# A fused attention and state-space kernel: the block hand-over spread over the chunks, weights scaled earlier, and attention's stages moved against the scans

## The chip, the cores and the metric

The kernel runs on one core of a Trainium2 chip. The metric is the device time of one execution in microseconds (us); below 0.2% two kernels of this kind can't be told apart. In the trace the engines are PE (matrix multiply), PEld (its weight loads), DVE (vector), ACT (activation functions), POOL (general purpose, elementwise here) and SP (which only issues DMA transfers here).

## What is computed

The input `x` is 8 samples of 512 channels by 48 x 48 = 2304 places, float32. Two layers follow one another, each of the form `x = x + layer(group_norm(x))`.

- Layer 0 is causal linear attention with 8 heads of 64 channels: `Q` and `K` are `elu(.) + 1` of linear maps of the input, `V` is a linear map; each place sums `k v^T` over all places up to it, multiplies by its `q`, and divides by `q` times the running sum of `k`.
- Layer 1 cuts the 512 channels into 4 blocks of 128 that depend on each other: a block's input is its own slice plus the output of the block before. Each block is a Mamba layer with 256 inner channels and 16 states: a convolution over 4 places with `silu`, a step size `delta = softplus(...)`, the recurrence `h = exp(delta*A)*h + delta*x*B` over 2304 places for every pair of channel and state, the output `sum(C*h)`, a gate `silu(z)` and a projection. Its result `x_m` is fused with the block's input `x_i`:

```
fused_global = max(x_i, x_m)
w_local, w_global = sigmoid(mean(x_i)), sigmoid(mean(fused_global))
fused = w_local * x_i + w_global * fused_global
```

The means run over all places, so a block's fusion can begin only when its last chunk is done, and the next block needs it.

## The kernel before

**Tiling.** 2304 places are 6 chunks of 384. One block of one sample over one chunk is a `Job`; there are 8 x 4 x 6 = 192. Two streams of jobs (even and odd samples) are interleaved in a fixed order, so that between the last chunk of a block and the first chunk of the next block of the same stream two jobs of the other stream run. A job is 8 slots. In a slot DVE makes the products of the next slot (`product`, L795) and runs 4 scans (`scan`, L816), each of 128 rows by 384 places; ACT makes for each scan the decay `exp(delta*A)` (`decay`, L805) in a bank of PSUM; POOL makes the last part of the products (`last_product`, L784) and multiplies the states by `C` (`weigh`, L832); PE sums them into one PSUM tile `yp` (`gather`, L839). The gather of a slot is issued in the middle of the second slot after it. After each half of the channels, in slot 6 and in slot 2 of the next job, DVE multiplies `yp` by the gate (`gated`, L851), and ACT starts `yp` anew (`skip`, L773).

**The order is written out at build time.** Every engine runs its own queue in program order. A planner counts half slots: `beside(half)` is called twice in each slot, before its first scan (even half) and after its second (odd half), and issues what is due from two lists of generators, attention's chunks (`heads`) and all the rest (`tasks`). Each `yield due, banks` says when the next stage may be issued (a number of halves after the last stage, or a fixed half) and how many of the 6 spare PSUM banks it needs; a stage that finds no banks slips to a later half. The decays take from the same 6 banks, 3 in advance (`DEPTH`), up to 5 ahead of silu and softplus. A bank freed by `free(late=True)` is *hot*: its last reader has been issued but is still to run; it is taken only where no other is spare, except by the decays.

**Three kinds of side work** lie beside the scans.

1. `Job.prepare`, once a job, begins 22 halves before the job's first slot: convolution (L624), gate (L635), four silu (L659 to L664), L670, L675, L683, two softplus (L694), POOL's `delta*xs` (L732), DMA loads. Exp, silu and softplus take different tables of ACT, so there is a table load on the way into silu and into softplus, and another back to exp.
2. `chunk(m)`, attention over one chunk, once for each job on the whole. `at(j)` is the half `times[m] + j`. Chunk c of a block has `times = 2 * first slot of the block's first job - BEFORE - (5 - c) * 16`, but at least 11 after the one before it (`DENSE`), and the first of all has `FIRST`. Its stages: projections (L279) at 0, 2 and 4; `q`, `k` (L334, L342); running key sums (L353); `pr` (L363); transposes (L370) at 9 and their copies (L374, L375) at 10; the state matmuls `ds` (L383) at 11 and their sums `S` (L392) at 12; the denominators `den` (L397), `rd` (L400, L402) at 13, `rdb` (L405) at 14; its transposes `rb` (L409) at 15; the product into `q` (L414) at 17; scores (L422) at 18; `sm` (L427) at 20; output matmuls at 21; L443 and L445 at 23. After a block's last chunk `group_norm` turns the statistics into a scale and a bias.
3. `pass_on`, once a block, runs when the block's last job has its maximum (L868). It takes the sums, gets the next block's place (`move_on`, which loads the weights and starts `scale_weights`: `wk` times `wi` on POOL, L493), computes the two sigmoids (L537 to L540, the sums at L549 and L552), and then fuses the 6 chunks one after another, each in 4 halves: ACT L579, L580, L584, POOL L589, L594, L597. The conv stage of a job waits in the planner until its chunk of the stream's input is ready and `st.scaled` is set.

Halves are counted below within a job: half 0 is the start of its slot 0, half 14 the start of its slot 7. Job starts are multiples of 16 halves, so stage `at(j)` of a chunk that isn't pushed by `DENSE` falls on half (j - BEFORE) modulo 16.

Of the kernel before, what the change touches and what calls it, by code (L numbers as in the profile page):

```python
# [9 lines left out]
F32 = mybir.dt.float32  # L10
# [6 lines left out]
P = 128  # L17
# [11 lines left out]
BEFORE, PERIOD, DENSE, FIRST = 62, 16, 11, -110  # L29
# [20 lines left out]
def attention_then_mamba_kernel(  # L50
# [111 lines left out]
    def group_norm(stats, n, name, bufs):  # L162


        bank = Banks()
        yield "1", 1
        mv = small.tile([P, n, 2], F32, tag=f"mv{n}", name=f"mv_{name}", bufs=1)
        for ct in range(n):
            nc.vector.bn_aggr(mv[:, ct, :], stats[:, ct].rearrange("p c s -> p (c s)"))
        mean_ps = bank()  # L170
        nc.tensor.matmul(mean_ps[:, 0:n], grp, mv[:, :, 0], start=True, stop=True)
        yield "1", 0
        gm = small.tile([P, 3, n], F32, tag=f"gm{n}", name=f"gm_{name}", bufs=1)
        nc.vector.tensor_copy(gm[:, 0, :], mean_ps[:, 0:n])
        bank.free()
        nc.vector.tensor_sub(gm[:, 1, :], mv[:, :, 0], gm[:, 0, :])
        nc.vector.tensor_mul(gm[:, 2, :], gm[:, 1, :], gm[:, 1, :])
        nc.vector.tensor_add(gm[:, 2, :], gm[:, 2, :], mv[:, :, 1])
        yield "0", 1
        var_ps = bank()  # L180
        nc.tensor.matmul(var_ps[:, 0:n], grp, gm[:, 2, :], start=True, stop=True)
        yield "1", 0
        nc.vector.tensor_scalar_add(gm[:, 2, :], var_ps[:, 0:n], 1e-5)
        bank.free()
        norm = small.tile([P, 3, n], F32, tag=f"norm{n}", name=f"norm_{name}", bufs=bufs)
        nc.gpsimd.tensor_tensor(norm[:, 0, :], gm[:, 2, :], power[:, 0:n], ALU.pow)
        yield "1", 0
        nc.vector.scalar_tensor_tensor(
            norm[:, 1, :], gm[:, 0, :], -1.0, norm[:, 0, :], ALU.mult, ALU.mult
        )  # L190
        nc.vector.scalar_tensor_tensor(
            norm[:, 2, :], gm[:, 1, :], float(L), norm[:, 0, :], ALU.mult, ALU.mult
        )
        return norm
# [64 lines left out]
    def chunk(m):  # L259
# [35 lines left out]
        if o == 0:  # L295
            yield at(-4), 0
            while b not in norms or m not in fetched:
                yield "1w", 0
            xn, norm = fetched.pop(m), norms[b]
            for ct in range(4):  # L300
                if ct:
                    yield at(ct - 4), 0
                nc.gpsimd.tensor_scalar(
                    xn[:, ct, :],
                    xn[:, ct, :],
                    norm[:, 0, ct : ct + 1],
                    norm[:, 1, ct : ct + 1],
                    ALU.mult,
                    ALU.add,
                )  # L310
            save(xns[b].rearrange("(t p) l -> p t l", p=P)[:, :, cols], xn)
        yield at(0), 1
# [64 lines left out]
        yield at(11), 1  # L377

        more = NT if c + 1 < NC else NT - 1
        ds = bank()[:, 0 : NT * 64].rearrange("p (i d) -> p i d", i=NT)  # L380
# [3 lines left out]
        yield at(12), 0  # L384
# [9 lines left out]
        yield at(12, 0), 1  # L394
        den = bank()[:, 0 : 2 * NT]
        for i in range(NT):
            nc.tensor.matmul(den[:, 2 * i : 2 * i + 2], pr[:, subs[i]], hsel, start=True, stop=True)  # L397
        yield at(13), 0
        rd = small.tile([P, 2 * NT], F32, tag="rd", name=f"rd_{n}", bufs=1)
        nc.vector.tensor_scalar_add(rd, den, 1e-10)  # L400
        bank.free()
        nc.vector.reciprocal(rd, rd)  # L402
        yield at(14), 0
        rdb = new("rdb", 1, (P, 2 * NT, 64))
        nc.scalar.copy(rdb, rd.unsqueeze(2).to_broadcast([P, 2 * NT, 64]))  # L405
        yield at(15), 1
# [5 lines left out]
        yield at(17), 0  # L412
# [5 lines left out]
        yield at(18), 2  # L418
# [4 lines left out]
        yield at(20), 0  # L423
# [6 lines left out]
        yield at(21), 1  # L430
# [11 lines left out]
        yield at(23), 0  # L442
# [9 lines left out]
    class Stream:  # L452


        def __init__(self, z, samples):
            self.z, self.samples = z, samples
            self.xi = cpool.tile([P, 3 + L], F32, name=f"xi_{z}")
            nc.gpsimd.memset(self.xi[:, 0:3], 0.0)
            self.b = None
            self.block = -1  # L460
            self.ready = 0

        def weights(self):

            n, z, s = self.n, self.z, self.s
            wi = wpool.tile([P, 512], F32, tag=f"wi{z}", name=f"wi_{n}")
            nc.sync.dma_start(out=wi, in_=win[s])

            wk = wpool.tile([P, 4, 256], F32, tag=f"wk{z}", name=f"wk_{n}")
            nc.sync.dma_start(  # L470
                out=wk.rearrange("p k d -> p (k d)"), in_=wconv[s].to_broadcast([P, 1024])
            )
            wo = wpool.tile([P, 2, P], F32, tag=f"wo{z}", name=f"wo_{n}")
            nc.sync.dma_start(out=wo, in_=wout[s])
            wx = wpool.tile([P, 2, 40], F32, tag=f"wx{z}", name=f"wx_{n}")
            nc.sync.dma_start(out=wx, in_=wxp[s])
            wd = wpool.tile([64, 256], F32, tag=f"wd{z}", name=f"wd_{n}")
            nc.sync.dma_start(out=wd[32:40, :], in_=wdt[s])
            nc.sync.dma_start(out=wd[40:41, :], in_=bdt[s])
            pv = wpool.tile([P, 4], F32, tag=f"pv{z}", name=f"pv_{n}")  # L480
            nc.sync.dma_start(out=pv[:, 0:2], in_=bconv[s])
            nc.sync.dma_start(out=pv[:, 2:4], in_=dskip[s])
            av = wpool.tile([P, 4, NS // 2], F32, tag=f"av{z}", name=f"av_{n}")
            nc.sync.dma_start(out=av, in_=alog[s])
            self.w = wi, wk, wo, wx, wd, pv, av

        def scale_weights(self):
            wi, wk, wo, wx, wd, pv, av = self.w
            yield "2", 0
            nc.scalar.activation(av, av, AF.Exp)  # L490
            for k in range(4):
                yield "1", 0
                nc.gpsimd.tensor_tensor(wk[:, k, :], wk[:, k, :], wi[:, 0:256], ALU.mult)  # L493
            nc.gpsimd.tensor_scalar_mul(av, av, -1.0)
            self.scaled = True

        def move_on(self):
# [15 lines left out]
            self.weights()  # L513
            self.scaled = False
            tasks.append(Task(self.scale_weights()))

        def pass_on(self):
# [25 lines left out]
            if not last:  # L543
                if self.fresh:
                    self.sums = norm[:, 2, :]
                else:

                    sums = small.tile([P, 2], F32, tag="sums", name=f"sums_{self.n}", bufs=3)
                    nc.vector.scalar_tensor_tensor(  # L549
                        sums[:, 0:1], wt[:, 2:3], wt[:, 0:1], norm[:, 2, :], ALU.mult, ALU.add  # L550
                    )
                    nc.vector.scalar_tensor_tensor(  # L552
# [18 lines left out]
            for c in range(NC):  # L571

                yield "1", 0
# [11 lines left out]
                if old is not None:  # L585
                    yield "1", 0
                    if c + 1 < NC:
                        now = loads(c + 1)
# [10 lines left out]
                else:  # L599
                    yield "1", 0  # L600
                    if c + 1 < NC:
                        now = loads(c + 1)
                self.ready = c + 1

    class Job:
# [6 lines left out]
        def prepare(self):  # L612
# [83 lines left out]
            yield "2", 0  # L696

# [192 lines left out]
    while min(count) < total:  # L890
# [3 lines left out]
        jobs.append(Job(streams[z], count[z], len(jobs) * SLOTS))  # L894
        count[z] += 1
# [200 lines left out]
    with tc.manual_schedule():  # L1096
        half_no[0] = FIRST - 6
        for st in streams:
            tasks.append(Task(st.pass_on()))
# [76 lines left out]
```

## Time and profile before

| | |
|---|---|
| time, median of 3 runs | 9815.3 us (9814.16 to 9816.18) |
| span of the profiled execution | 9811.4 us |
| granted PE clock, mean | 0.905 of full speed |
| DMA, mean | 167 GB/s |
| scans, L816 | 6144 of 941 ns, 5508.1 us |
| products, L795 | 1536 of 1197 ns, 1838.9 us |
| weighing by C, L832 (POOL) | 1536 of 3176 ns, 4878.7 us |
| last products, L784 (POOL) | 1954.2 us |
| decays, L805 (ACT) | 6144 of 580 ns, 3441.7 us |
| ACT table loads, L805, L659 and L694 | 382 + 192 + 192 of 1283 ns |

How to read the profile: its page gives for each engine the time in which it was busy, then 40 equal slices of the span, the DMA queues, the chain of work that ended last, and the costliest groups of instructions by line. Beside the page the trace answers questions: the list of waits names an engine's instruction, whom it waited for, the time in total, how often, and the longest; the groups by shape give busy time and mean of each line; the timeline lists instructions in order of time (start, length, engine, line, operation, operands, how many were merged, and in brackets the idle time ahead of it and who ended it). Neighbouring instructions overlap by some 0.1 us, so busy times of an engine add up to a little more than the time they take.

### The profile page before, as it was taken

How to read it: one execution, taken by the hardware profiler on the slowest of the kernel's cores; microseconds unless marked ns; L12 is line 12 of the kernel's file. 1: busy time of each engine (PE TensorE's matmuls, PEld its weight loads, DVE VectorE, ACT ScalarE, POOL GpSimd, SP SyncE). 2: the span in 40 equal slices, each digit the busy share in tenths (PEclk: the TensorE clock that was granted, in tenths of full speed). 3: DMA queues.
4: the chain of work that ended last, by engine and by line, in shares of the span. 5: the costliest groups of instructions: out<-in, count | busy, mean ns of one | idle time of the engine just before them, and what ended most of it. 6: DMA issues, size and time to landing. Idle time of an engine off the chain costs nothing.

```text
span 9811.4 us, 120393 instructions
## 1 busy us (share of the span) xinstructions
PE 8005.0 (82%) x35714; PEld 3805.1 (39%) x35714; DVE 8465.1 (86%) x11624; ACT 6630.3 (68%) x12624; POOL 8108.8 (83%) x5667
## 2 busy tenths in 40 slices
PE   7888888878888888887888888888888888888865
PEld 4433433333333334333333333433333433334322
DVE  4888888889888888888988888888888888888888
ACT  3666676666776667666677666666666676666666
POOL 3788888888888888888888888888888888888899
PEclk9999999999999999988999999998899999999987
DMA  6566566666666555666666665557666656655555
GB/s 199 154 164 165 160 165 168 171 171 183 175 170 171 160 161 158 169 172 183 177 170 172 167 166 161 161 159 184 179 182 167 165 163 167 170 160 156 163 151 138
DMA packets 1002897, 1642.82 MB, mean 167 GB/s; under 512 B 138592, under 2 KB 797312, under 8 KB 1002240
## 3 DMA queue, kind: packets, MB, share of 16 engines
q1 hardware_dynamic: 1002240, 1635.13, 60.9%
q8 instruction: 282, 4.62, 0.2%
q14 instruction: 375, 3.07, 0.1%
HBM read 1309.06 MB, written 325.58 MB: 167 GB/s over the span
## 4 chain that ended last, share of the span: by engine, by line
DVE 31%; PE 23%; ACT 15%; POOL 11%; issue 9%; DMA 9%; SPq 2%; POOLq 0%; DVEq 0%; ACTq 0%
DVE u L816 20%; PE bank L279 10%; POOL u L832 6%; ACT bank L805 6%; PE yp L839 5%; DVE u L795 5%; PE bank L624 2%; DMA dxr<-xscr 2%; ACT L694 2%; POOL u L784 2%; DMA C<-scr 2%; SPq L724 1%; PE bank L635 1%; PE bank L409 1%; ACT L659 1%
## 5 line engine op out<-in xcount | busy, mean ns | idle before, releaser
L816 DVE TENSOR_TENSOR_SCAN u<-bank,u 128x385 f32<-128x385 f32 (+1 forms) x6144 | 5508.1, 941 | 270.2 <-ACT bank L805 268.6
L832 POOL TENSOR_TENSOR u<-u,C 128x1536 f32<-128x1536 f32 x1536 | 4878.7, 3176 | 463.6 <-DVE u L816 283.7
L805 ACT ACTIVATE bank<-dr,av 128x385 f32<-128x385 f32 (+1 forms) x6144 | 3441.7, 580 | 1618.9 <-DVE u L816 1235.1
L839 PE MATMUL yp<-u,cst 128*64 128x384 f32 x12288 | 2486.2, 527 | 493.7 <-ACT yp L773 264.9
L784 POOL TENSOR_TENSOR u<-B,dxr 128x512 f32<-128x512 f32 x1536 | 1954.2, 1272 | 39.1 <-PE yp L839 24.4
L279 PE MATMUL bank<-xn,wq_sb 128*128 128x384 f32 x4608 | 1908.5, 565 | 20.2 <-DVE fg L868 10.7
L795 DVE TENSOR_TENSOR u<-B,dxp 128x1024 f32<-128x1024 f32 x1536 | 1838.9, 1197 | 13.9 <-ACT dxp L768 11.8
L839 PEld LDWEIGHTS yp<-u,cst 128*64 128x64 f32 x12288 | 797.6, 142 | 1632.2 <-issue 1078.7
L624 PE MATMUL bank<-xi,wk 128*128 128x384 f32 x3072 | 1191.4, 534 | 210.7 <-DVE u L816 162.7
L279 PEld LDWEIGHTS bank<-xn,wq_sb 128*128 128x128 f32 x4608 | 982.3, 224 | 759.3 <-issue 258.7
L830 POOL COPY state<-u 128x4 f32<-128x4 f32 x1280 | 240.9, 188 | 932.0 <-DVE u L816 846.7
L624 PEld LDWEIGHTS bank<-xi,wk 128*128 128x128 f32 x3072 | 603.0, 207 | 854.3 <-DVE u L816 336.7
L291 ACT ACTIVATE ex<-bank,bqkv_sb 128x384 f32<-128x384 f32 x384 | 222.9, 580 | 757.4 <-PE bank L279 738.6
L409 PE MATMUL bank<-cst,rdb 128*128 128x128 f32 x576 | 157.3, 405 | 593.0 <-ACT delta L694 588.9
L851 DVE TENSOR_TENSOR yz<-yp,sz 128x384 f32<-128x384 f32 x384 | 213.3, 556 | 372.6 <-PE yp L839 372.4
L805 ACT ACT_TABLE_LOAD x382 | 490.1, 1283 | 6.7
L732 POOL TENSOR_TENSOR delta<-delta,xs 128x384 f32<-128x384 f32 x384 | 384.1, 1000 | 105.9 <-DMA dscr<-delta 84.4
L635 PE MATMUL bank<-xi,wi 128*128 128x384 f32 x768 | 339.5, 532 | 152.8 <-ACT xs L659 152.8
L392 DVE TENSOR_TENSOR S<-S,bank 128x64 f32<-128x64 f32 x512 | 112.8, 220 | 321.0 <-ACT sz L664 155.6
L348 ACT ACTIVATE vT<-bank,bqkv_sb 128x384 f32<-128x384 f32 x192 | 111.4, 580 | 403.0 <-PE bank L279 403.0
L409 PEld LDWEIGHTS bank<-cst,rdb 128*128 128x128 f32 x576 | 89.1, 196 | 712.9 <-ACT delta L694 684.5
L857 PE MATMUL bank<-yz,wo 128*128 128x384 f32 x768 | 322.6, 542 | 29.2 <-DVE yz L851 12.0
(112 smaller groups left out, 8328.7 us busy)
## 6 DMA issues: line engine op xcount, KB each, us to landing
B<-scr SPq DMA_DIRECT2D x1536, 192.0 KB
C<-scr SPq DMA_DIRECT2D x1536, 192.0 KB
xn<-xn SPq DMA_DIRECT2D x192, 768.0 KB
dr<-dscr SPq DMA_DIRECT2D x768, 192.0 KB
dxr<-xscr SPq DMA_DIRECT2D x768, 192.0 KB
dscr<-delta SPq DMA_DIRECT2D x192, 384.0 KB
xscr<-delta SPq DMA_DIRECT2D x192, 384.0 KB
xn<-in_x SPq DMA_DIRECT2D x48, 768.0 KB
```

Source lines behind the costliest of these rows:

```text
L279: nc.tensor.matmul(ps, wq_sb[:, kt, j * 512 + o * P : j * 512 + (o + 1) * P], xn[:, kt, :], start=(kt == 0), stop=(kt == 3),)
L409: nc.tensor.transpose(rb[:, i, :], rdb[:, 2 * i : 2 * i + 2, :].rearrange("p e d -> p (e d)"), ident)
L624: nc.tensor.matmul(xc, wk[:, k, h * P : (h + 1) * P], xi[:, c0 + k : c0 + k + LC], start=(k == 0), stop=(k == 3),)
L635: nc.tensor.matmul(zp, wi[:, 256 + h * P : 256 + (h + 1) * P], xi[:, c0 + 3 : c0 + 3 + LC], start=True, stop=True,)
L732: nc.gpsimd.tensor_tensor(delta[:, h, :], delta[:, h, :], xs[:, h, :], ALU.mult)
L784: nc.gpsimd.tensor_tensor(u[:, :, :, 1 + LC - TAIL :], self.B[s % 4][:, :, cols].unsqueeze(2).to_broadcast(shape), self.dxr[s // 4][:, :, ...
L795: nc.vector.tensor_mul(u[:, :, :, 1 : 1 + LC - TAIL], self.B[s % 4][:, :, cols].unsqueeze(2).to_broadcast(shape), self.dxp.unsqueeze(1).to ...
L805: nc.scalar.activation(dA[:, cols], self.dr[h][:, g, cols], AF.Exp, scale=self.w[6][:, 2 * h + g, q + j : q + j + 1],)
L816: nc.vector.tensor_tensor_scan(u[:, j, g, cols], dA[:, cols], u[:, j, g, cols], 0.0, ALU.mult, ALU.add,)
L832: nc.gpsimd.tensor_tensor(h, h, self.C[s % 4].unsqueeze(2).to_broadcast([P, NG, 2, LC]), ALU.mult)
L839: nc.tensor.matmul(self.yp[g * 64 : g * 64 + 64, 0:LC], pair_sum, u[:, j, g, 1:], start=False, stop=(s % 4 == 3 and j == NG - 1), skip_gro ...
L857: nc.tensor.matmul(self.xm[:, 0:LC], self.w[2][:, h, :], self.yz[:, h, :], start=(h == 0), stop=(h == 1),)
```

## The change

It has four parts.

1. **Blocks fused chunk by chunk.** `pass_on` no longer runs through the 6 chunks in a burst. From the second chunk on it loads a chunk 36 halves and fuses it 30 halves ahead of the job that needs it; the loads of one chunk are no longer issued while the one before is worked on.
2. **Weights scaled early.** `weights` becomes a task of its own that loads and scales the next block's weights. It starts when the last job of a block has issued its softplus, and not when the block is over. Three tiles that are still in use by then (`wo`, `pv`, `av`) get a second buffer; the multiplication of `av` by -1 goes from POOL to ACT.
3. **Column products with scalars.** In `group_norm` and `pass_on`, products of one column by another (`tensor_mul`, `scalar_tensor_tensor` with two column tensors) become `tensor_scalar`, with the second column as a scalar for each partition. For 4 columns there are 4 such instructions.
4. **Attention's places.** `BEFORE` goes from 62 to 61 and `FIRST` from -110 to -115, so a chunk lies one half later against the jobs. `den` and `ds` go into one bank, in one stage at 12; `rd` and `S` follow in one stage at 14; everything from `rdb` on is one half later again. A new wait at the head of a chunk keeps it behind the chunk two before it.

```diff
-BEFORE, PERIOD, DENSE, FIRST = 62, 16, 11, -110
+BEFORE, PERIOD, DENSE, FIRST = 61, 16, 11, -115
...
-        nc.vector.tensor_mul(gm[:, 2, :], gm[:, 1, :], gm[:, 1, :])
-        nc.vector.tensor_add(gm[:, 2, :], gm[:, 2, :], mv[:, :, 1])
+            nc.vector.tensor_scalar(
+                gm[:, 2, :], gm[:, 1, :], gm[:, 1, :], mv[:, 0, 1:2], ALU.mult, ALU.add
+            )
...
-        nc.vector.scalar_tensor_tensor(
-            norm[:, 1, :], gm[:, 0, :], -1.0, norm[:, 0, :], ALU.mult, ALU.mult
-        )
...
+        for i, factor in ((0, -1.0), (1, float(L))):
+            for ct in range(n):
+                nc.vector.tensor_scalar(
+                    norm[:, 1 + i, ct : ct + 1],
+                    gm[:, i, ct : ct + 1],
+                    norm[:, 0, ct : ct + 1],
+                    factor,
...
+        while read[0] < m - 1:
+            yield "1w", 0
         yield at(0), 1
...
-        yield at(11), 1
+        yield at(12), 1
+        both = bank()
+        den = both[:, 0 : 2 * NT]
+        for i in range(NT):
+            nc.tensor.matmul(den[:, 2 * i : 2 * i + 2], pr[:, subs[i]], hsel, start=True, stop=True)
...
-        yield at(12), 0
+        yield at(14), 0
+        rd = small.tile([P, 2 * NT], F32, tag="rd", name=f"rd_{n}", bufs=1)
+        nc.vector.tensor_scalar_add(rd, den, 1e-10)
+        nc.vector.reciprocal(rd, rd)
...
-        yield at(14), 0
+        yield at(15), 0
         rdb = new("rdb", 1, (P, 2 * NT, 64))
...
-        yield at(15), 1
+        yield at(16), 1
         rb = bank()[:, 0:LC].rearrange("p (i t) -> p i t", i=NT)
...
-            nc.gpsimd.tensor_scalar_mul(av, av, -1.0)
+            nc.scalar.mul(av, av, -1.0)
             self.scaled = True
...
-            self.weights()
-            self.scaled = False
-            tasks.append(Task(self.scale_weights()))
+            self.w = self.coming
...
-                yield "1", 0
+                if c and not last:
+                    first = 2 * self.jobs[self.block * NC + c].start
+                    yield (first - 36, 1), 0
+                    now = loads(c)
+                    yield (first - 30, 1), 0
...
+            if c == NC - 1 and (st.s < 3 or st.samples):
+                tasks.append(Task(st.weights()))
```

## The prediction

> **What bounds the kernel now.** I began with the busy shares on the page, because they tell whether there is a single bound.
>
> ```profile
> PE 8005.0 (82%) x35714; PEld 3805.1 (39%) x35714; DVE 8465.1 (86%) x11624; ACT 6630.3 (68%) x12624; POOL 8108.8 (83%) x5667
> ```
>
> DVE, POOL and PE are all above 80%, so none of them has much to spare. DVE is the fullest, and an average job confirms its lead: 192 jobs of 51 us, of which scans and products take 38. So the question is what DVE waits for. Next I read DVE's rows in the list of waits (total us, times, longest).
>
> ```profile
> DVE yz L851 <- PE yp L839: 372.4, 158, 5.0
> DVE u L816 <- ACT bank L805: 268.6, 234, 5.0
> DVE S L392 <- ACT sz L664: 155.6, 90, 3.9
> DVE S L392 <- PE bank L383: 153.1, 60, 4.4
> ...
> DVE q L414 <- PE bank L409: 92.1, 150, 2.5
> ```
>
> All of DVE's rows together come to some 1280 us, 13% of the span; these five (and S at L390, 37 us) are 1080 of it. Then I cut the timeline at each L795 into slots and averaged. A slot that holds nothing but its product and four scans takes 4.55 us (8 x 4.55 = 36.4 for a job); slot 7 takes 7.56 and slot 2 takes 8.47. An ordinary job takes 46.7 to 47.5 us. Three of every six are longer, 51.5, 52.4 and 54.9 us: the job whose attention chunk is the last of its block, then the job in which a stream's block is handed over, then the one after. Slots 7 to 2 of an ordinary job, in four views of the timeline:
>
> ```profile
> 1396.94 1.81 DVE L816 TENSOR_TENSOR_SCAN u<-bank,u 128x385 f32<-128x385 f32 x2
> 1400.01 0.73 DVE L392 TENSOR_TENSOR S<-S,bank 128x64 f32<-128x64 f32 x3 [1.26 <-ACT sz L664]
> 1401.85 0.96 DVE L816 TENSOR_TENSOR_SCAN u<-bank,u 128x385 f32<-128x385 f32 x1 [0.25 <-ACT bank L805]
> ...
> 1417.04 0.56 DVE L851 TENSOR_TENSOR yz<-yp,sz 128x384 f32<-128x384 f32 x1 [2.56 <-PE yp L839]
> ```
>
> ```profile
> 1399.94 1.28 ACT L805 ACT_TABLE_LOAD   x1
> 1401.23 1.09 ACT L805 ACTIVATE bank<-dr,av 128x385 f32<-128x385 f32 x2
> ...
> 1409.55 0.87 ACT L694 ACTIVATE delta<-bank 128x384 f32<-128x384 f32 x2
> ```
>
> ```profile
> 1410.09 0.90 PE L409 MATMUL bank<-cst,rdb 128*128 128x128 f32 x3 [3.94 <-ACT delta L694]
> 1410.79 4.76 PE L279 MATMUL bank<-xn,wq_sb 128*128 128x384 f32 x8
> 1415.48 1.51 PE L839 MATMUL yp<-u,cst 128*64 128x384 f32 x8
> ```
>
> The third fence is the important one. The transposes `rb` stand in PE's queue in a bank that softplus still reads (the planner found only hot ones), so PE is blocked 3.94 us; behind them come a projection of 4.76 us and only then the gather that DVE's `yz` waits for. In the first two, `S` waits for the silu block, since `ds` slipped to banks that silu frees.
>
> **What the Trainium skill says.** "SBUF — State Buffer", section "Who interferes with whom": a DVE instruction with two SBUF inputs and a POOL instruction that reads SBUF exclude each other for a whole instruction. The trace agrees: one column costs over 1 us in the first two rows and 160 ns in the next, same engine, same size, once the way is free.
>
> ```profile
> L188 DVE SCALAR_TENSOR_TENSOR norm_m<-gm_m,norm_m 128x1 f32<-128x1 f32 x32 | 37.9, 1185 | 12.2 <-POOL norm_m L186 12.2
> L177 DVE TENSOR_TENSOR gm_m<-gm_m 128x1 f32<-128x1 f32 x32 | 37.0, 1157 | 1.1
> ...
> L178 DVE TENSOR_TENSOR gm_m<-gm_m,mv_m 128x1 f32<-128x1 f32 x32 | 5.1, 160 | 1.1
> ```
>
> "VectorE: DVE Perf Modes", "What auto-detection actually checks": an instruction with one source may also use both ports, where both sides lie in SBUF and the size is even or equal. The trace has a `tensor_scalar` of two columns within SBUF (L539) at 399 ns, and one that reads PSUM (L400) at 155. "ScalarE: Activation LUTs", "What ACT_TABLE_LOAD costs": 1283 ns and a drain of about 1380 more. The load agrees; the drain doesn't show, as the decay at 1401.23 starts when the load at 1399.94 ends. "PSUM — Partial Sum Buffer", "Engine vs sequencer instructions": matmuls start and complete in program order; that is the third fence.
>
> **The change part by part.**
>
> *Attention's places: rb and yz.* Prepare begins at -22, so silu falls on half 14 and softplus on half 18 = 2. A chunk starts at (0 - 62) mod 16 = 2; `rb` at 15 would be half 1, but `ds` and `S` slip by one behind silu and `rb` lands on half 2 with softplus. Now the chunk starts on 3, nothing of it wants a bank on half 14, `rb` falls on 16 + 3 = half 3, after two scans have freed banks that aren't hot, and the projection leaves half 2 with it. The gather due in the middle of slot 1 then stands ahead of both. Waits of 372 (yz) and 92 (q) are at stake. A hand-over's first chunk runs later and may still meet softplus, so I keep 80: **-384**.
>
> *Attention's places: S.* This looks like 345 us and is, in ordinary jobs, nothing. Six banks less three for silu leave three decays; the fourth scan of slot 7 needs one made after silu and its table load. ACT has it at 1401.8 whatever DVE does meanwhile. Without `S` the third scan runs at 1398.7 and the fourth still at 1401.85: the wait changes its name to L816 <- L805. And the sums, 0.65 us in 171 chunks, now hidden there, lie open in slot 0: **+110**. `rd` stays in slot 0, the other stages only change slots: 0. One projection, `ds` and `den` on other halves cost PE nothing, as it idles between. The copies `kl`, `v` come just ahead of silu on ACT, with decays queued behind; ACT waits 0.3 us twice there, which hides most of it.
>
> *Hand-over: weights and spreading.* Now `scaled` is set at half 11, the new block's first conv comes at half 13 and its silu on half 0 of the next job, behind a burst that repeats every 4 halves (ACT 0.6 + 0.6 + 0.7, POOL 3 x 1.0). DVE pays, in the two jobs:
>
> ```profile
> 1249.50 0.73 DVE L392 TENSOR_TENSOR S<-S,bank 128x64 f32<-128x64 f32 x3 [4.36 <-PE bank L383]
> ...
> 1262.64 0.96 DVE L816 TENSOR_TENSOR_SCAN u<-bank,u 128x385 f32<-128x385 f32 x1 [5.04 <-ACT bank L805]
> ```
>
> Against 47.3 us these two jobs lose 5.1 + 7.5 = 12.6 us, 30 times: 378. With weights ready the conv comes at half 12; chunk 0 still has to be fused first and POOL's column power, ready waits and one late silu stay. I take 8 of the 12.6: **-240**. The scaling itself (POOL 4 x 0.73 a block) only moves.
>
> *Spread fusions, the new wait.* A fusion 30 halves ahead falls on half 2, and its ACT part (0.6 + 0.6 + 0.7, 1.77 net) is issued ahead of softplus. Behind softplus on ACT is the decay of slot 2's first scan; DVE's scan waits for it. By my count of the queue the decay then ends some 0.4 us too late, in the 160 jobs with chunk 1 to 5: **+64**. Bounds: 0 if hidden, 1.77 x 160 = 283 if not at all.
>
> *Column products.* L177 32 x 1.0, L188 32 x 1.03, L549 24 x 0.81, L178 and L552 7: 92 if each new one takes 0.16 as L400 does; at L539's 0.40, 120 x 0.24 = 29 less. One column has no two halves to use both ports for; **-90**. With 4 columns 8 of 0.155 replace 1.4 + 0.15: 0.
>
> *Less room.* At 9375 us POOL would be 86% busy and PE 85%. In the tail, where no attention is left, jobs take 40.2 us and POOL is 96% busy (busy times of the engines from 9500 to 9700 us, a stretch of 200):
>
> ```profile
> sum 200.00, PE 139.46 PEld 52.89 DVE 187.64 ACT 144.57 POOL 191.72; mean PE 139.46 PEld 52.89 DVE 187.64 ACT 144.57 POOL 191.72
> ```
>
> So POOL can follow, but jobs with fusions (3 us) and normalisations (2.6 us) get tight, and fusions now meet POOL's `delta*xs` on halves 3 to 6, which the transfers of `xscr` await. For queueing I add **+100** (0 to 200). Sum: -384 + 110 - 240 - 90 + 64 + 100 = -440, so **9375**.
>
> **The rivals.** *All of it:* no yz or q wait is left (-464), hand-overs are as ordinary jobs (-378), columns -90, `S` +110, the rest 0: 8993. For it: PE's projection takes 4.76 us after a wait and 2.85 elsewhere, so fewer waits may speed PE too; against it: three full engines. *Waits that take the place of waits:* half of the first (-192) and of the hand-overs (-120), +110, -90, +64, +55: 9642. For it: `S` is such a case already, and 738 us of ACT waiting for projections may surface as late decays. *Slower:* yz keeps its wait (0), now for POOL late with fusions; every fusion delays a scan in full (+283), +110, -240, -90: 9878. For it: L839 already waits 198 us for POOL's L832 and L784; against it: POOL idles 1 to 2 us in most slots of an ordinary job.
>
> **How the numbers follow.** Forecast 0.58, all of it 0.10, waits for waits 0.22, slower 0.07, within 0.2% 0.03. The range 9120 to 9720 leaves out most of the second (0.08), the top of the third (0.02), slower and same: 0.20. Faster 0.90, same 0.03, slower 0.07.
>
> **What would show it.** Right: L851 <- L839 under 100 us; L409 no longer behind L694; L392 without waits and L816 <- L805 grown to some 500; L177's and L188's successors near 160 ns; the jobs at a hand-over near 49. Wrong: L851 waiting as before behind POOL, or L816 <- L805 beyond 800, or column products still at 1 us.

## The result, and the profile after

The changed kernel takes 9325.3 us (median of 4 runs, 9319.0 to 9332.9) against 9814.7 before: a ratio of 0.9502, 95% interval 0.9485 to 0.9518. The forecast was 9375 in a range of 9120 to 9720. Lines have moved: the scan L816 is now L830, the product L795 is L809, the decay L805 is L819, `yz` L851 is L865, `rb` L409 is L418, `S` L392 is L410, the projections L279 are L288, the gather L839 is L853, softplus L694 is L705, silu L659 is L670.

First the busy shares on the page of the changed kernel, again DVE, POOL and PE together near the top:

```profile
PE 7735.1 (83%) x35714; PEld 3673.0 (39%) x35714; DVE 8348.4 (90%) x11640; ACT 6580.2 (71%) x12656; POOL 8080.8 (87%) x5635
```

DVE was busy for 8465 of 9811 us and idle for 1346; now it is busy for 8348 of 9322 and idle for 973. So of the 490 us of the two spans, 373 are idle time and 117 are work. DVE's rows in the list of waits of the changed kernel (total us, times, longest):

```profile
DVE u L830 <- ACT bank L819: 503.2, 194, 4.7
DVE q L345 <- ACT bank L301: 141.5, 63, 6.6
DVE k L353 <- ACT bank L301: 70.8, 144, 2.3
...
DVE yz L865 <- PE yp L853: 9.7, 7, 4.9
...
DVE q L423 <- PE bank L418: 3.8, 1, 3.8
```

The waits of `yz` and of the product into `q` went from 464 us to 13. No row for `S` is left, but the scan's wait for its decay went from 269 to 503. The features `q` and `k` now wait 212 us for ACT, where they waited 32 before. Put to the jobs in which they fall, 113 of these 212 us lie in the second job of a hand-over and 48 ahead of the first scan, so ordinary jobs have little of them. PE in an ordinary job, from slot 0 to slot 2 (slot 1 from 1365.98, slot 2 from 1370.51, read from the starts of L809):

```profile
1364.35 1.51 PE L853 MATMUL yp<-u,cst 128*64 128x384 f32 x8
1368.19 0.52 PE L418 MATMUL bank<-cst,rdb 128*128 128x128 f32 x3 [2.33 <-DVE u L830]
1368.95 2.85 PE L288 MATMUL bank<-xn,wq_sb 128*128 128x384 f32 x8 [0.24 <-DVE u L830]
```

Compare the order with the fence of before: the gather now runs ahead of `rb` and of the projection. In this job `rb` waits for two scans to free its bank and no longer for softplus (over the whole kernel 86 us of that wait are left, in 28 cases, against 589), and the projection takes 2.85 us and not 4.76. It is the same work on the same operands. What differs is the clock that PE was granted, as a share of full speed the third figure from the end of each row below (a row gives the busy time of each engine in one stretch). The first row is the stretch of the kernel before in which PE's wait of 3.94 us ends and the projection runs; the second is the stretch of the changed kernel with the rows of the fence above:

```profile
1408.10:1414.80 6.70, 4.71 (x10) 2.86 (x11) 5.73 (x7) 4.28 (x7) 5.46 (x4) 0.50 1.06 280
1364.30:1372.00 7.70, 5.13 (x22) 2.61 (x21) 7.70 (x10) 7.28 (x12) 6.79 (x7) 1.00 0.99 251
```

So one collision cost twice. PE stood still for 3.94 us, its granted clock fell to half before that wait was over, and so the projection ahead of the gather took 1.9 us longer as well. By these lines some 1.9 of the 2.56 us for which `yz` waited in that job are the slow projection (an estimate: 4.76 less 2.85). It is no single case: of the 147 times in the trace of before at which `rb` waits over 1 us for softplus and the projection's 8 matmuls follow, the clock was at half for over 1 us of the projection in all 147, and the projection took 4.76 us in the median. In the changed kernel's view PE waits 2.33 us at this place, and the clock stays full.

Slot 7 of that job, DVE and then ACT:

```profile
1353.86 2.65 DVE L830 TENSOR_TENSOR_SCAN u<-bank,u 128x385 f32<-128x385 f32 x3
1359.67 0.96 DVE L830 TENSOR_TENSOR_SCAN u<-bank,u 128x385 f32<-128x385 f32 x1 [3.16 <-ACT bank L819]
```

```profile
1352.50 0.48 ACT L385 COPY kl<-bank 128x384 f32<-128x384 f32 x1
1352.88 0.49 ACT L386 COPY v<-bank 128x384 f32<-128x384 f32 x1
1353.25 1.10 ACT L819 ACTIVATE bank<-dr,av 128x385 f32<-128x385 f32 x2
1354.37 1.28 ACT L670 ACT_TABLE_LOAD   x1
...
1357.76 1.28 ACT L819 ACT_TABLE_LOAD   x1
1359.05 1.09 ACT L819 ACTIVATE bank<-dr,av 128x385 f32<-128x385 f32 x2
```

Three scans run without a pause, then the fourth waits 3.16 us for the first decay after silu. The two copies stand directly ahead of silu, so the slot now takes 7.8 us and not 6.9. Cut at L809 as before, ordinary jobs went from 46.7 to 47.5 us down to 46.3 to 46.5, and the three long ones (51.5, 52.4 and 54.9) to 46.2, 44.8 and 52.6. These are medians. Added up over all jobs, the differences from the kernel before show where the time was gained, here and in five of the runs below (us; the last column is what lies ahead of the first slot, the first four jobs, the last five, and what comes after):

| | ordinary jobs (92) | attention's last chunk (30) | first job of a hand-over (30) | second (30) | start and end |
|---|---|---|---|---|---|
| changed kernel | -80 | -153 | -209 | -92 | +43 |
| column products alone | -2 | -46 | -36 | -1 | -8 |
| places alone | -88 | -154 | -114 | +43 | +18 |
| hand-over alone | +71 | +21 | -102 | -130 | +25 |
| weights early alone | +40 | +4 | -92 | +23 | -2 |
| changed, half a slot earlier | +197 | -35 | -129 | -116 | +47 |

Only 80 of the 490 us come from ordinary jobs, which the views above show; 454 come from the three jobs around the end of a block, and the start and the end have become 43 us longer. In the ordinary jobs slots 1 to 3 became 310 us shorter together and slots 4 to 6 106 longer, in part because stages moved from the ones to the others; slot 0 became 56 us longer and slot 7 70.

### The profile page after: what moved, and what is told of

Its sections match the earlier page's. It is cut to its first block, busy times and chain, and to the rows that moved or that the text cites. A ratio compares the mean times of both kernels' runs of the same rounds, so it can differ in the third digit from the quotient of the medians.

```text
span 9321.5 us, 120629 instructions
## 1 busy us (share of the span) xinstructions
PE 7735.1 (83%) x35714; PEld 3673.0 (39%) x35714; DVE 8348.4 (90%) x11640; ACT 6580.2 (71%) x12656; POOL 8080.8 (87%) x5635
## 4 chain that ended last, share of the span: by engine, by line
DVE 39%; ACT 20%; PE 18%; issue 7%; DMA 7%; POOL 6%; SPq 2%; DVEq 0%; POOLq 0%; ACTq 0%
DVE u L830 23%; DVE u L809 8%; PE bank L288 7%; ACT bank L819 6%; PE bank L635 4%; POOL u L846 4%; ACT L819 3%; PE yp L853 3%; PE bank L646 2%; ACT L705 2%; DMA B<-scr 2%; DMA C<-scr 1%; ACT bank L301 1%; ACT delta L705 1%; DVE sm L436 1%
## 5 line engine op out<-in xcount | busy, mean ns | idle before, releaser
L830 DVE TENSOR_TENSOR_SCAN u<-bank,u 128x385 f32<-128x385 f32 (+1 forms) x6144 | 5475.1, 938 | 530.5 <-ACT bank L819 503.2
L819 ACT ACTIVATE bank<-dr,av 128x385 f32<-128x385 f32 (+1 forms) x6144 | 3431.3, 579 | 1556.9 <-DVE u L830 1113.3
L853 PE MATMUL yp<-u,cst 128*64 128x384 f32 x12288 | 2429.9, 514 | 282.7 <-ACT yp L787 146.3
L288 PE MATMUL bank<-xn,wq_sb 128*128 128x384 f32 x4608 | 1855.1, 552 | 48.8 <-DVE u L830 31.7
L809 DVE TENSOR_TENSOR u<-B,dxp 128x1024 f32<-128x1024 f32 x1536 | 1834.7, 1195 | 10.7 <-ACT dxp L782 10.7
L853 PEld LDWEIGHTS yp<-u,cst 128*64 128x64 f32 x12288 | 788.3, 139 | 1476.6 <-issue 903.5
L635 PE MATMUL bank<-xi,wk 128*128 128x384 f32 x3072 | 1118.2, 507 | 280.1 <-ACT kl L385 172.7
L288 PEld LDWEIGHTS bank<-xn,wq_sb 128*128 128x128 f32 x4608 | 929.1, 212 | 862.9 <-issue 215.1
L635 PEld LDWEIGHTS bank<-xi,wk 128*128 128x128 f32 x3072 | 563.7, 193 | 862.2 <-ACT kl L385 254.1
L844 POOL COPY state<-u 128x4 f32<-128x4 f32 x1280 | 243.8, 190 | 740.6 <-DVE u L830 738.0
L787 ACT ACTIVATE yp<-xs,pv 128x384 f32<-128x384 f32 x384 | 223.4, 582 | 405.7 <-DVE yz L865 405.7
L418 PE MATMUL bank<-cst,rdb 128*128 128x128 f32 x576 | 112.7, 310 | 426.1 <-DVE u L830 334.7
L694 PE MATMUL bank<-dbc,wd 9*128 9x384 f32 x768 | 316.3, 524 | 65.1 <-ACT dbc L686 29.0
L646 PE MATMUL bank<-xi,wi 128*128 128x384 f32 x768 | 297.8, 500 | 59.8 <-ACT xs L670 59.8
L449 PE MATMUL bank<-sm,v 128*64 128x128 f32 x2304 | 257.2, 301 | 42.4 <-DVE u L830 40.6
L418 PEld LDWEIGHTS bank<-cst,rdb 128*128 128x128 f32 x576 | 66.8, 153 | 558.9 <-ACT xb L601 272.5
```

What stands on the lines that cost most here:

```text
L288: nc.tensor.matmul(ps, wq_sb[:, kt, j * 512 + o * P : j * 512 + (o + 1) * P], xn[:, kt, :], start=(kt == 0), stop=(kt == 3),)
L635: nc.tensor.matmul(xc, wk[:, k, h * P : (h + 1) * P], xi[:, c0 + k : c0 + k + LC], start=(k == 0), stop=(k == 3),)
L646: nc.tensor.matmul(zp, wi[:, 256 + h * P : 256 + (h + 1) * P], xi[:, c0 + 3 : c0 + 3 + LC], start=True, stop=True,)
L694: nc.tensor.matmul(vp, wd[32:41, h * P : (h + 1) * P], dbc[32:41, :], start=True, stop=True)
L809: nc.vector.tensor_mul(u[:, :, :, 1 : 1 + LC - TAIL], self.B[s % 4][:, :, cols].unsqueeze(2).to_broadcast(shape), self.dxp.unsqueeze(1).to ...
L819: nc.scalar.activation(dA[:, cols], self.dr[h][:, g, cols], AF.Exp, scale=self.w[6][:, 2 * h + g, q + j : q + j + 1],)
```

## The experiments

All were timed beside the kernel before on the same chip; ratios are to it, with 95% intervals. The number to compare them with is the changed kernel's 0.9502 (0.9485 to 0.9518).

**Each part alone.** Three kernels carry one part of the change each, cut from the diff shown above.

*Column products:* the hunks in `group_norm` and for `sums`. Among them is a line that the diff above leaves out: the subtraction for `gm` takes the mean from PSUM and no longer from its copy in SBUF (144 ns and not 241).

> The kernel before with the column products alone (tensor_scalar with a column as scalar). Main theory (a column product with two column tensors waits for POOL, one with a scalar doesn't): 88 long instructions fall from about 1.1 us to 0.16 to 0.27, some 80 to 90 us in all: 9725 to 9735. Rival (DVE had time to spare at these places, other waits fill it): within 20 us of 9815.

Measured 9719.6 us, 0.9904 (0.9891 to 0.9918): 94 us less. The instructions, in the groups by shape of this kernel (busy us, mean ns):

```profile
L195 DVE TENSOR_SCALAR norm_m<-gm_m,norm_m 128x1 f32<-128x1 f32 x64 | 9.9, 196 | 0.0
L178 DVE TENSOR_SCALAR gm_m<-gm_m,mv_m 128x1 f32<-128x1 f32 x32 | 8.7, 273 | 1.2
L558 DVE TENSOR_SCALAR sums<-wt,norm_m 128x1 f32<-128x1 f32 x24 | 6.6, 273 | 0.9
```

They were 1185, 1157 and 969 ns. DVE is busy for 92 us less (8372.6 against 8465.1), and its waits add up to the same as before: all of the saved work was on the path.

*Attention's places:* `BEFORE`, `FIRST` and the hunks in `chunk`.

> The kernel before with attention's places alone (BEFORE 61, FIRST -115, den and ds in one stage, all later stages one half later). Main theory: the waits of yz and q (464 us in before) go, S loses its wait but the fourth scan of slot 7 waits instead, and the sums lie open: 9815 less 200 to 300, so 9515 to 9615, with L392's wait at 0 and the scan's wait for ACT above 500 us. Rival (the places matter only together with the smooth hand-over): 9700 or more.

Measured 9517.2 us, 0.9697 (0.9684 to 0.9710): 296 us less, the largest part. The scan's wait is 523 us, as expected, and no wait of `yz` or `S` is among the first rows:

```profile
DVE u L816 <- ACT bank L805: 523.0, 212, 4.6
DVE rd L392 <- PE bank L389: 101.5, 30, 3.7
DVE q L336 <- ACT bank L292: 85.8, 86, 7.5
```

Its ordinary jobs take 45.9 to 46.5 us. With the burst still in place, the second job of a hand-over remains long, 56 us. But the first fell from 52.4 to 47.8: in the kernel before, the sums `S` waited there for PE, 117 us over all such jobs, and that wait is gone with the places alone. So the jobs around a block's end, and not the ordinary ones, hold most of the 296 us.

*The hand-over:* all the hunks in `Stream`, in `prepare` and at the end.

> The kernel before with the hand-over alone (fusions spread over the chunks, weights loaded and scaled early). Main theory: the two jobs after a block's end lose their 12.6 us, 30 times: 9815 less 200 to 350, so 9465 to 9615; ordinary jobs stay at 47 us or get slower by up to 1, as each now has a fusion. Rival (the spread fusions cost in ordinary jobs what they save at the hand-over): above 9700.

Measured 9697.7 us, 0.9881 (0.9867 to 0.9894): 116 us less, outside what the main theory expected and at the edge of the rival's range. The jobs show why. The two jobs of a hand-over fell from 52.4 and 54.9 to 48.2 and 50.2, over all of them by 232 us. But ordinary jobs went up from 47.2 to 47.9, since most of them have a fusion now; with the jobs of attention's last chunks that is 92 us, and 25 more at the start and the end. The fusion stands on half 2 ahead of softplus, on which `rb` is still waiting in this kernel:

```profile
DVE yz L856 <- PE yp L844: 310.3, 157, 5.0
DVE q L414 <- PE bank L409: 225.9, 155, 2.5
```

The product into `q` waits 226 us against 92 before. So both theories hold a part: the hand-over gains what was expected of it, and half of that is given back elsewhere.

The three parts give 94 + 296 + 116 = 506 us, together 489: they add up to within 17 us. By kind of job they do not: ordinary jobs gain 61 us more together than the three parts have it, which fits fusions that cost little once `rb` no longer waits behind them, and the three jobs around a block's end gain 65 less.

*Weights early, without the spreading:* the hunks in `weights`, `move_on` and at the end.

```diff
-            self.weights()
-            self.scaled = False
-            tasks.append(Task(self.scale_weights()))
+            self.w = self.coming
...
+            if c == NC - 1 and (st.s < 3 or st.samples):
+                tasks.append(Task(st.weights()))
```

> The kernel before with the weights alone loaded and scaled early; the fusions still come in a burst. Main theory (the hand-over costs both because the first conv waits a half for scaled weights and because of the burst): about half of the 9 us a block that the hand-over alone gained in its two jobs, so 9815 less 100 to 200: 9615 to 9715, and ordinary jobs stay at 47.2, since no fusion lies in them. Rival (the burst is the whole cost): 9790 or more.

Measured 9787.1 us, 0.9973 (0.9964 to 0.9983), 27 us less: in the time nearly what the rival expected. The table shows that the small number hides two larger ones. The first job of a hand-over gains 92 us, nearly as much as with the spreading (102); the second loses 23, and ordinary jobs lose 40, mostly in slot 2, where `yz` waits 413 us and not 372. So it isn't that scaling cost little: early weights relieve the first job, and the spreading the second, which gains 130 with both. Why ordinary jobs get slower here was not isolated.

**Does S cost what its wait says?** One edit to the kernel before moves the sums into slot 0 and leaves the rest.

```diff
-        for i in range(more):
-            if c == 0 and i == 0:
-                nc.vector.tensor_copy(S[:, place[1], :], ds[:, 0, :])
...
         nc.vector.tensor_scalar_add(rd, den, 1e-10)
-        bank.free()
         nc.vector.reciprocal(rd, rd)
+        place = range(NT + 1) if c % 2 == 0 else range(NT, -1, -1)
+        for i in range(more):
...
+        bank.free(2)
```

> The kernel before with one edit: the sums S are issued in the stage of rd, in slot 0, and no longer in slot 7. Main theory (slot 7 is as long as ACT's silu block with its table loads lets it be, and S only hid in it): the 345 us of S waiting for silu turn into scans waiting for ACT, and the sums, about 0.65 us in 171 chunks, now lie open: no gain, 9815 to 9925. Rival (the wait of S is DVE's loss, as the list of waits has it): 9470 to 9650.

Measured 9849.7 us, 1.0037 (1.0024 to 1.0050). The 345 us of `S` are gone from the list, and this stands at its top:

```profile
DVE u L815 <- ACT bank L804: 617.7, 235, 5.7
DVE yz L850 <- PE yp L838: 343.2, 158, 4.9
DVE rd L393 <- PE bank L390: 107.7, 40, 5.2
```

The scan's wait is 269 + 349. In ordinary jobs slot 7 is 6.9 us as before, so there the wait only changed its name. That 349 is so near to 345 is in part chance: in the first job of a hand-over it is `rd` that now waits for PE (107.7 us in all, 20.6 before). The sums lie open in slot 0, which became 86 us longer over all jobs, but slot 2 gave 34 of it back, as `yz` there waits less. So the kernel is only 36 us slower.

**Which half?** The changed kernel, one half earlier:

```diff
-BEFORE, PERIOD, DENSE, FIRST = 61, 16, 11, -115
+BEFORE, PERIOD, DENSE, FIRST = 62, 16, 11, -116
```

> The changed kernel with its chunks one half earlier again (BEFORE 62, FIRST -116), so that rb and a projection fall near softplus's half; everything else stays. Main theory (the half in which rb and the projection stand against softplus decides whether the gather, and with it yz, waits): the projection at half 2 takes hot banks again, yz waits 150 to 350 us in all and the time rises by 100 to 300 from 9325. Rival (it was ds, S and den that mattered, or the smooth hand-over): within 50 us of 9325.

Measured 9775.7 us, 0.9961 (0.9949 to 0.9974). Half a slot takes back 450 of the 489 us, more than the main theory expected.

```profile
DVE yz L865 <- PE yp L853: 665.2, 160, 5.5
DVE u L830 <- ACT bank L819: 387.0, 187, 4.7
```

`yz` waits longer than in the kernel before (372), because now `rb`, at 16, is on softplus's half by the plan, behind ACT's fusions, with the projection ahead of the gather. Slot 2 went from 6.9 to 11.4 us in ordinary jobs (medians), and by 590 us over all jobs, which is more than the whole loss. Yet slot 7 of its ordinary jobs takes 6.9 us again. Its copies of `kl` and `v` are on half 12, ahead of slot 7, and ACT's table load for silu starts 0.72 us after the slot does, as in the kernel before; in the changed kernel it starts 1.62 us after (medians of ordinary jobs). The block from there to the end of the load back to exp takes 4.67 us in all three. That names the copies as what made slot 7 longer in the changed kernel.

**Can slot 7 be made shorter?** Three kernels try it.

```diff
             turned.append(ps)
-        yield at(10), 0
+        yield at(9, 0), 0
         kl, v = new("kl", 1, (P, NT, P)), new("v", 2, (P, NT, P))
```

> The changed kernel with the copies of kl and v issued in half 12, with their transposes, and not in half 13. Main theory (slot 7 grew from 6.9 to 7.8 us because these two copies, 0.9 us, stand on ACT right ahead of silu): the scan's wait in slot 7 falls from 3.1 to about 2.3 us, 0.8 in some 150 jobs: 9325 less 80 to 130, so 9195 to 9245. Rival (silu waits for its convolution or for banks, and the copies fill idle time): 9300 or more.

Measured 9443.8 us, 0.9621 (0.9608 to 0.9634): 118 us slower than the changed kernel. A miss. The transposes are issued in the same half and PE isn't done with them; ACT stands still with `skip` and the decays behind the copies:

```profile
ACT kl L385 <- PE bank L381: 244.6, 152, 6.7
...
ACT v L386 <- PE bank L381: 176.8, 116, 1.9
...
ACT xs L673 <- PE bank L635: 142.6, 89, 3.0
```

Slot 6, in which ACT stands still, is no longer than in the changed kernel. DVE pays in slot 7, 9.0 us and not 7.8, and the last row says why: the table load does start earlier, 0.92 us into the slot, but then the second silu waits for its convolution on PE, and the block takes 6.55 us and not 4.67. In one such job PE had waited 1.49 us for `pr` and 1.15 for `skip`, its granted clock was 0.50 from 2813.1 to 2816.4, and the convolution took 3.95 us, against 2.85 at full clock in the changed kernel:

```profile
2812.18 2.05 PE L853 MATMUL yp<-u,cst 128*64 128x384 f32 x8 [1.15 <-ACT yp L787]
2814.16 3.95 PE L635 MATMUL bank<-xi,wk 128*128 128x384 f32 x8
```

Next, silu's inputs in two banks, so that a fourth decay fits:

```diff
-            yield "2", 2
+            yield "2", 1
             xc1 = conv(1)
-            zp0 = gate(0)
...
             bank.free()
-            zp1 = gate(1)
+            zp0 = gate(0)
             nc.scalar.activation(xs[:, 1, :], xc1, AF.Silu, bias=pv[:, 1:2])
+            bank.free()
+            zp1 = gate(1)
...
-            bank.free(3, late=True)
+            bank.free(2, late=True)
```

> The changed kernel with silu's four inputs in two banks: each gate's matmul is issued after the silu that frees its bank, so one more bank is left for decays in slot 7. Main theory (the fourth scan of slot 7 waits because only three decays fit beside silu's three banks): a fourth decay is ready, slot 7's wait of 3.1 us loses 0.5 to 1.0, in some 150 jobs 9325 less 60 to 140. Rival (ACT's queue is late anyway, and the gates now wait for silu): 9310 or more.

Measured 9342.4 us, 0.9516 (0.9503 to 0.9529): no difference from the changed kernel. Slot 7 did fall, from 7.8 to 4.5 us. But slot 0 rose from 5.4 to 7.8, its first scan waiting:

```profile
1350.53 1.81 DVE L831 TENSOR_TENSOR_SCAN u<-bank,u 128x385 f32<-128x385 f32 x2 [2.54 <-POOL u L847]
1352.25 0.14 DVE L401 TENSOR_SCALAR rd<-bank 128x6 f32<-128x6 f32 x1
```

ACT's first decay after silu started at 1349.86 and took 0.59 us, and that scan followed at 1350.53. The releaser named, POOL, is the other semaphore of the scan; by the times it was the decay. Around silu ACT itself is the bound, and an additional decay in advance mostly shifts where DVE pays. The silu block also grew, from 4.67 to 5.32 us, as the gates now wait for the silu that frees their bank. The two slots together are still 0.9 us shorter in ordinary jobs, but these gain only 18 us in all against the changed kernel; the second job of a hand-over gains 108, and attention's last chunk and the first job of a hand-over lose 78 and 73.

Then both, with the transposes one half earlier:

```diff
-        yield at(9), 0
-        pr = new("pr")
-        nc.vector.tensor_mul(pr, q, kc)
-        bank.free()
-        yield at(9, 0), 2
+        yield at(8, 0), 2
         turned = []
...
-        yield at(10), 0
+        yield at(9), 0
+        pr = new("pr")
+        nc.vector.tensor_mul(pr, q, kc)
+        bank.free()
```

> The kernel of silu_two_banks, and in it the transposes of k and vT one half earlier (half 11), their copies on half 12. Main theory (the two copies right ahead of silu cost slot 7 its 0.9 us; in copies_half_12 they only waited for their own transposes): a further 0.6 to 0.9 us in 150 jobs, 90 to 130 us below silu_two_banks, the best of all kernels, near 9150. Rival (three banks more at half 11 and 12 starve the decays of slots 5 and 6): no faster than silu_two_banks.

Measured 9436.0 us, 0.9614 (0.9600 to 0.9627), 94 us slower than with two banks alone: the rival. The copies' cost did go: in ordinary jobs the table load for silu starts 0.72 us into slot 7, as in the kernel before. But slot 7 still takes 7.5 us, since the block takes 5.32, as with two banks alone. Ordinary jobs take 45.6 to 46.5 us, but the jobs at a hand-over rise to 48.3 and 54.2, where `rd` waits, and the list has 157 us of such waits. That is not the starved slots 5 and 6 which the rival named; which of the moved stages holds the banks is open.

**Where should a fusion stand?** The changed kernel with the spread fusion 4 halves later, then 2 halves earlier (the loads with it):

```diff
-                    yield (first - 36, 1), 0
+                    yield (first - 32, 1), 0
                     now = loads(c)
-                    yield (first - 30, 1), 0
+                    yield (first - 26, 1), 0
```

> The changed kernel with each spread fusion 4 halves later (26 halves ahead of its job, on half 6 and no longer on softplus's half 2). Main theory (the fusion's 1.8 us on ACT ahead of softplus delay the decay behind it and the features): 0.3 to 0.5 us in 160 jobs, 9325 less 40 to 90. Rival (POOL, 87% busy, is loaded worse at halves 7 to 9, or the fusion comes too late for the next conv): 9325 or more.

Measured 9638.6 us, 0.9823 (0.9810 to 0.9837): 313 us slower than the changed kernel. A miss, far beyond the rival's number:

```profile
ACT dxp L782 <- DMA dxr<-xscr: 173.8, 84, 6.7
```

The transfers of `xscr` come late for `dxp`, which comes ahead of a product of DVE (127 us of waits there; 11 in the changed kernel). In the list of SP's waits the stores wait 998 us for POOL's L844, a row that isn't among the first of the changed kernel. So SP's queue may have held the loads up behind a store; that reading fits, but it wasn't isolated, and much of that row stands in place of other waits of the same stores. Nor is it the whole loss: the scans' wait for their decays grew from 503 to 660 us as well. By slots the loss lies mostly in 6 and 7, which became 134 and 97 us longer. With `first - 38` for the loads and `first - 32` for the fusion:

> The changed kernel with each fusion 2 halves earlier, on half 0 (32 ahead), between silu and softplus. Main theory after fusion_half_6 (what a fusion costs depends on what queues behind it: on half 6 to 9 it made POOL's products, the xscr transfer and so dxr late): here nothing of that is behind it, and ACT is just done with silu, so the wait of features falls but slot 0 and 1 may wait for decays: 9325 less 50 to plus 50. Rival (any place away from half 2 upsets the transfers): 9500 or more.

Measured 9285.6 us, 0.9462 (0.9449 to 0.9475): 40 us better than the changed kernel, and the intervals do not meet. The features wait 177 us and not 212, and most of that change lies in the second job of a hand-over.

**One column or two?** One addition of two columns was left (`wt`, 751 ns in the changed kernel). On top of the last kernel:

```diff
-                nc.vector.tensor_scalar_add(wt[:, 0:2], wt[:, 0:2], 1.0)
+                for i in range(2):
+                    nc.vector.tensor_scalar_add(wt[:, i : i + 1], wt[:, i : i + 1], 1.0)
```

> The kernel of fusion_half_0 with one more edit: the addition of 1 to the two columns of wt (0.75 us in the changed kernel) becomes two instructions of one column. Main theory (an even size within SBUF lets a tensor_scalar use both ports, for which it waits for POOL; one column doesn't): each of the two takes 0.16 to 0.27 us, 10 to 15 us in all, which the time can hardly show: 9265 to 9285. Rival (it waits for POOL whatever its size): one of the two takes 0.7 us or more.

Measured 9265.9 us, 0.9442 (0.9429 to 0.9455), the fastest of all kernels here, and 0.6% below the changed kernel. Groups by shape, first with two columns (the kernel of `fusion_half_0`), then with one:

```profile
L546 DVE TENSOR_SCALAR wt<-wt 128x2 f32<-128x2 f32 x32 | 23.6, 737 | 0.3 <-ACT wt L544 0.3
```

```profile
L547 DVE TENSOR_SCALAR wt<-wt 128x1 f32<-128x1 f32 x64 | 6.6, 144 | 0.3 <-ACT wt L544 0.3
```

One instruction of two columns takes 0.74 us in the mean, two of one column are done in 0.21, as they overlap. The means hide a wide spread: the 32 instructions of two columns in the changed kernel took between 170 and 1868 ns, and none of the 64 of one column took more than 153. That is 17 us of work; the time moved by 20, but the intervals of the two kernels overlap.

## Why the prediction was right, point by point

- **rb and yz (-384): right in the mechanism, with one part of it missing.** 464 us of waits fell to 13, and the places alone gave -296, where the sum put -384, +110 for `S` and nothing of its own for slot 7: -274. That `softplus_half_again` loses 450 us for half a slot, all of it and more in slot 2, shows that the mechanism is the order of PE's queue against softplus, as the third fence of the prediction had it. What it had only in a rival, as a projection that is slower after a wait, is PE's clock: it was at half when the projection ran, and in the view shown that made up most of `yz`'s wait. One collision costs more in the changed kernel, as ACT's fusions now stand ahead of softplus too (PE waits 4.72 us there in one view). And most of the gain isn't in the ordinary jobs that the argument was made on: the places alone gave 88 us in these, and 268 in the job of attention's last chunk and the first of a hand-over.
- **S is worth nothing in ordinary jobs (0, and +110 for the open sums): right.** Slot 7 of ordinary jobs stayed at 6.9 us in `sums_late`. The open sums made slot 0 longer by 86 us there, of which `yz`'s wait took up 34; in the changed kernel, where `yz` hardly waits, slot 0 is 56 us longer in the 92 ordinary jobs, 0.6 a job, near the 0.65 that was counted. But in the first job of a hand-over `S` waited 117 us for PE, and that went with the places; the prediction had it under the hand-over.
- **Copies ahead of silu ("which hides most of it"): wrong.** They were given nothing; slot 7 of ordinary jobs went from 6.9 to 7.8 us with the copies ahead of silu, and back to 6.9 where `softplus_half_again` put them a half earlier. That is 0.9 us in most jobs. The idle time of 0.3 us that the prediction saw on ACT sits between decays that wait for the scans' banks, and there was too little of it.
- **Hand-over (-240): the sum close, its division not.** The two jobs gave 232 us where handed over alone. In the changed kernel 107.3 fell to 97.4 us, near the 98 (twice 49) that was named, but neither job is near 49: the first takes 44.8, helped by the places, and the second 52.6. The weights alone gave 92 us in the first job and took 23 in the second.
- **Spread fusions (+64): right in sign; the size is not shown.** In the kernel before, with `rb` still behind softplus, they cost some 0.7 us an ordinary job. With the places moved they cost little there: slot 2 of the 92 ordinary jobs is 10 us longer in all than with the places alone, some 0.1 us a job and not the 0.4 that was counted. Moving them off softplus's half gains 40 us, more than half of it in the second job of a hand-over.
- **Column products (-90): right**, 94 us, though each takes 0.20 to 0.27 us and not 0.16. "VectorE: DVE Perf Modes", "What auto-detection actually checks", names, for one source and both sides in SBUF, an even or equal size as the condition for the second port. That a single column falls outside it was the prediction's own reading; the last experiment agrees with it in the times, 737 against 144 ns, but shows no ports.
- **Less room (+100): not seen as such.** POOL went from 83 to 87% busy, and DVE has almost no wait for it. What came in its place wasn't in the sum: the features' wait for ACT grew by 180 us, some 100 of them already with the places alone, and the start and the end became 43 us longer.

So that the sum came within 50 us of the measured change is in part luck: too much for less room, and nothing for slot 7, the features, the start and the end. The direction, and the mechanism of the largest term, were not luck.

## What to carry to other kernels

Where engines run queues in order, look for a long wait on an engine that has time to spare, and read what stands behind it: PE's 3.9 us behind softplus cost DVE its wait only because a gather came later in the same queue, and a good part of it only because the clock had fallen in the meantime. A wait in the list is worth its time only if nothing else ends at the same moment; before you count it, ask when the next instruction could have run without it, which here was ACT's first decay after its table load. And work that is spread evenly isn't free: each piece needs a place with nothing urgent queued behind it, and here half a slot was worth 450 us in one place, and two slots 313 us in another.

## What the runs showed of the hardware

A `tensor_scalar` on two columns within SBUF took 0.17 to 1.87 us in the changed kernel, 751 ns in the mean (399 in the kernel before, 737 with the fusions on half 0), and one on a single column 127 to 153 ns. That POOL is what the slow ones waited for is the prediction's reading; the trace names no one.

PE's projection of 8 matmuls took 2.85 us at a granted clock of 1.00 and 4.76 at 0.50, after PE had waited 3.94 us. After a wait of 2.33 us the clock was still 1.00. Over the whole kernel the mean of these matmuls went from 565 to 552 ns and that of `rb` from 405 to 310, at a mean granted clock of 0.948 and not 0.905. So in this kernel taking out PE's waits made its work shorter too.
